# An order written by a planner: when scores, maxima and products with v take their turn on TensorE

## The chip, the cores and the metric

The kernel runs on one core of one Trainium2 chip. The metric is the device time of one execution in microseconds (us), as the median of several runs. The engines are named as in the profile: PE is TensorE (PEld its weight loads), DVE is VectorE, ACT is ScalarE, POOL is GpSimd, SP is SyncE, which here only issues DMAs.

## The reference

```python
xn = layernorm(x)                                  # x: (2, 2048, 256) float32
q = rope((xn @ wq).reshape(B, S, 16, 16))          # 16 heads of 16
k = rope((xn @ wk).reshape(B, S, 4, 16))           # 4 heads of keys and values
v = (xn @ wv).reshape(B, S, 4, 16)
k, v = repeat(k), repeat(v)                        # 4 query heads to each
scores = einsum('bshd,bthd->bhst', q, k) / 4, causal
out = einsum('bhst,bthd->bshd', softmax(scores), v) @ wo
y = real(ifft(fft(xn) @ (w_real + 1j * w_imag))) + bias
result = x + out + y
```

Everything is float32. The spectral term is a fixed 256 x 256 matrix, which the kernel builds once.

## The kernel before

The 4096 rows of x are cut into eight blocks of 512 rows (block n is batch n % 2, block row j = n // 2). A block has four *units* of four query heads each, 32 units in all. Unit u of block row j runs over 4 (j + 1) *steps*, one for every 128 keys; there are 320 steps. The work of a unit is of three kinds:

- *Maxima* (called "A" in the code, tiles `sm`). Before a softmax can be formed, the maximum of each row of scores is needed. PE multiplies queries by keys with the queries as weights (L155 for whole tiles, L627 and L631 with the causal mask), two heads to a tile of two PSUM banks, and DVE takes the maximum (`mx`, L636). There are two such tiles (`ps_s`, bufs=2). After a unit's last maximum, DVE splits the negated maxima into three bf16 parts (`parts`, L656), PE turns them (`spread`, "S", tile `ps_m`, L671), ACT copies them to `mt` (L677) and issues a DMA (L678) that puts them under the queries in `qst`, so that the next product subtracts the maximum by itself.
- *Scores* ("B", tiles `st`). PE multiplies again, with keys as weights (L155; L716 and L720 with the mask), one head at a time, four to a step, each into one PSUM bank. ACT takes the exponential into `es` in SBUF (L726). On the diagonal, POOL sets the masked part to zero (L729). There are three `st` banks (`ps_st`, bufs=3), and all smaller results that PE passes on (projections, turned tiles, outputs) go through the same three. `es` has 8 places, two to a step, so scores can be four steps ahead of the products.
- *Products with v* ("V", tile `av`, L757). For each step, four heads at once add to one PSUM bank (`ps_av`, bufs=1). `va` has a column of ones, so the sum of the exponentials comes along. After the last step of a unit ACT copies `av` to `avs` (`take`, L768), and only then can the next unit's first product begin. DMAs on the POOL queue then regroup the heads through DRAM (`put`, `gather`, `widen`), DVE inverts the sums and POOL scales.

Beside them stand the *pieces*: each block's load, row statistics, norm, turned rows (`ps_x`, L411), projections (`ps_q`, L155, evacuated by ACT at L427), rotation and split on POOL (L518 to L556), the DMAs that stack the parts into `qst` and `kst` (SP, L393), and each block's outputs (`po`, L155, added by DVE at L883). Each piece has a step from which it may be placed and a step by which it is due.

The order of all engines is written out at build time by a planner (`while True`, from L1070). It holds a clock for each engine (`clock`) and the time at which each value or free buffer is there (`there`), with costs for each operation: 0.22 us for a full score on PE and 0.49 on ACT, 0.87 for a product, 1.14 for a full maximum on DVE. At each turn it collects what could go next on PE, with the planned time at which it could begin (`at`). The choices that could begin within 0.05 us of PE's clock are in `soon`. A score needs a free `st` bank and, for the first of a pair, a free place in `es`. A maximum needs a free `sm` tile, and may be no more than six tiles (`WINDOW`) beyond those due at the next step. A piece that is due is "F", one that is not is "M". Then it picks:

```python
        act, dve = clock["act"] - pe, clock["dve"] - pe
        lag = now - v_next
        late = a_done < due[min(now, NS)]
        if not soon:
            pick = min(choices, key=lambda c: (c[0], "AFSBVM".index(c[1])))
        elif half and "A" in soon:
            pick = soon["A"]
        elif "S" in soon:
            pick = soon["S"]
        elif late and "A" in soon:
            pick = soon["A"]
        elif "F" in soon:
            pick = soon["F"]
```

`act` and `dve` are the work that ACT and DVE still have before them when PE comes to this turn; `lag` is how many steps the scores are ahead of the products. The branches that follow are those of the change, below. Each engine then runs its own list in the order in which it was written, and waits on semaphores for what it needs.

Of the kernel before, what the change touches and what calls it, by code (L numbers as in the profile page):

```python
# [23 lines left out]
def tile_attn_plus_spectral_ffn(  # L24
# [32 lines left out]
    B = x.shape[0]  # L57
# [42 lines left out]
    def take_slot(tag):  # L100
        used[tag] += 1
        return used[tag] - 1
# [5 lines left out]
    def ready(needs):  # L108

        if any(k not in there for k in needs):  # L110
            return None
        return max((there[k] for k in needs), default=0.0)
# [623 lines left out]
    def values_need(u, t):  # L736
        n, g = units[u]
        b, j = blocks[n]
        return [
            ("es", u, t, 0), ("es", u, t, 1), ("va", at_block[b, t // NI]), ("av", u - 1),  # L740
            *[("avs", u - 2)] * (t == (j + 1) * NI - 1),
        ]

    def values(u, t):
        n, g = units[u]
        b, j = blocks[n]
        nt = (j + 1) * NI
        if t == 0:
            av[u] = ps_av.tile([P, SB], F32, tag="av", name=f"av{u}")
            take_slot("av")  # L750
        lo = max(0, t - j * NI) * P
        use(
            "pe", (SB - lo) * 1.68e-3 + 0.01, values_need(u, t),
            [("es", es_slot[u, t, pr]) for pr in range(2)] + [("values", u)],
        )
        for h in range(NKV):
            nc.tensor.matmul(  # L757
                av[u][QD * h : QD * (h + 1), lo:],
                va[at_block[b, t // NI]][:, t % NI, h, :],
                es[u, t, h // 2][:, h % 2, lo:],  # L760
                start=(t == 0), stop=(t == nt - 1),
            )
# [3 lines left out]
    def take(u):  # L766
        avs[u] = work.tile([P, SB], F32, tag="avs", bufs=3, name=f"avs{u}")
        nc.scalar.copy(avs[u], av[u])  # L768
        take_slot("avs")
        use("act", 0.47, [("values", u), ("avs", u - 2)], [("av", u), ("avs", "in", u)])  # L770
# [125 lines left out]
    AHEAD = (3, 5, 5, 5)  # L896
    RATE = (1.4, 1.2, 1.12, 1.1)
    WINDOW = 6
    FULL = 0.7
    steps = [(u, t) for u, (n, g) in enumerate(units) for t in range((blocks[n][1] + 1) * NI)]  # L900
    first = {}
    for at, (u, t) in enumerate(steps):
# [41 lines left out]
    k = take_slot("st")  # L944
# [118 lines left out]
    def wants(needs, rings):  # L1063
        return [*needs, *(slot(*SECOND.get(tag, (tag, 0))) for tag in rings)]

    def start_of(eng, needs, rings=()):
        t = ready(wants(needs, rings))
        return None if t is None else max(t, clock[eng])

    while True:  # L1070
        now = b_next // NKV
        pe = clock["pe"]
        choices = []

        if now < NS:
            u, t = steps[now]
            h = b_next % NKV
            n, g = units[u]
            at = start_of(
                "pe", [("mt", n, g), ("kst", at_block[blocks[n][0], t // NI])],  # L1080
                ["st"] + ["es"] * (h % 2 == 0),
            )
            if at is not None:
                choices.append((at, "B", None))

        if v_next < NS and v_next < now:
            at = start_of("pe", values_need(*steps[v_next]))
            if at is not None:
                choices.append((at, "V", None))

        if a_done < len(a_list):
            at = pe if half else start_of("pe", a_list[a_done][2], ["s"])
            if at is not None and a_done < due[min(now + 1, NS)] + WINDOW:
                choices.append((at, "A", None))
        if spread_next < len(units) and ("np", *units[spread_next]) in there:
            at = start_of("pe", [("np", *units[spread_next])], ["st"])
            if at is not None:
                choices.append((at, "S", None))
        others = []
        for s in streams:  # L1100
            if s and (s[0][0] <= now or now >= NS):
                since, by, eng, needs, rings, what = s[0]
                at = start_of(eng, needs, rings)
                if at is None:
                    continue
                if eng == "pe":
                    choices.append((at, "F" if by <= now else "M", s))
                else:

                    if by <= now and ready(wants(needs, rings)) <= clock[eng] < pe + 1:  # L1110
                        at = min(at, pe)
                    others.append((at, s))
        limit = max(pe, min((c[0] for c in choices), default=1e9))
        if others and min(others, key=lambda c: c[0])[0] <= limit:
            soonest = min(others, key=lambda c: c[0])
            eng = soonest[1][0][2]
            s = min(
                (c for c in others if c[0] <= soonest[0] + 0.1 and c[1][0][2] == eng),
                key=lambda c: c[1][0][1],
            )[1]  # L1120
            s.pop(0)[-1]()
            continue
        if not choices:
            break
        soon = {}
        for c in choices:
            if c[0] <= pe + 0.05 and (c[1] not in soon or c[0] < soon[c[1]][0]):
                soon[c[1]] = c
# [10 lines that stand above are left out]
            pick = soon["A"]  # L1139
        elif "F" in soon:  # L1140
            pick = soon["F"]
        elif "B" in soon and act < FULL and (act <= dve or "A" not in soon):
            pick = soon["B"]
        elif "A" in soon and dve < FULL:
            pick = soon["A"]
        elif "V" in soon and lag > 1:
            pick = soon["V"]
        else:
            pick = next(soon[k] for k in "MVBA" if k in soon)
        kind = pick[1]  # L1150
        if kind == "B":
            scores(*steps[now], b_next % NKV)
            b_next += 1
            u, t = steps[now]
            if b_next % NKV == 0 and first[u + 1] == now + 1:
                n, g = units[u]
                there["qst", 2 + NG * n + g] = clock["pe"]
        elif kind == "V":
            values(*steps[v_next])
            v_next += 1  # L1160
            u = steps[v_next - 1][0]
            if first[u + 1] == v_next:
                take(u)
        elif kind == "A":
            one, two, needs, parts = a_list[a_done]
            (two if half else one)()
            if half:
                a_done += 1
                if parts:
                    parts()  # L1170
            half = not half
        elif kind == "S":
            made[spread_next][2]()
            spread_next += 1
        else:
            pick[2].pop(0)[-1]()
# [51 lines left out]
```

## Time and profile before

| | |
|---|---|
| median of 3 runs | 945.44 us (944.21 to 949.61) |
| profiled execution | 948.13 us, its span 946.4 us |
| granted PE clock | 0.996 |
| PE, DVE, ACT, POOL busy | 912.4, 751.8, 670.0, 370.8 us |
| scores on ACT (L726) | 1280 of 539 ns (mean of four widths) |
| maxima on DVE (L636) | 640 of 1058 ns (mean of four widths) |

The page of the profile gives busy time by engine, the busy share and the granted PE clock in 40 slices of the span, and the costliest groups of instructions. In a group's row, the first number after the bar is its busy time, the next the mean duration of one in ns, and after the second bar stands the time for which its engine was idle just before such instructions, with what ended most of that. [...]records of consecutive matmuls overlap, and four matmuls of 32 columns each run side by side.

### The profile page before, as it was taken

The numbers are of one execution on the slowest core, as the hardware profiler recorded it, in microseconds if no ns is written. First come the engines' busy times: TensorE is split into PE (matmuls) and PEld (weight loads), VectorE is DVE, ScalarE is ACT, GpSimd is POOL, SyncE is SP. The second block draws the span as 40 slices with busy tenths as digits, with TensorE's granted clock in tenths as the row PEclk, the third lists the DMA queues.
The fourth block names the chain that finished last, engine by engine and source line by source line (L and its number), as shares of the span: only waits on it lengthen the run. The fifth ranks groups of instructions, "written<-read, shape, count | busy, mean of one in ns | idle before, by whom it ended". The sixth has DMA issues, their size and how long they took to land.

```text
span 946.4 us, 39041 instructions
## 1 busy us (share of the span) xinstructions
PE 912.4 (96%) x17324; PEld 516.3 (55%) x17324; DVE 751.8 (79%) x1056; ACT 670.0 (71%) x1418; POOL 370.8 (39%) x556
## 2 busy tenths in 40 slices
PE   8998899999999999999999999999999999999996
PEld 5665665656565555655554555565456455555442
DVE  7777787789779995898897899879788887888511
ACT  3266555687667775888856777858688885888884
POOL 6397746825762324821337420302561031102201
PEclk9999999999999999999999999999999999999999
DMA  5436633350262011440012500010152001100000
GB/s 167 112 100 154 167 89 93 99 144 26 74 162 69 25 38 42 117 121 14 26 37 62 146 27 14 27 58 14 47 124 52 14 24 41 34 2 29 11 2 23
DMA packets 41993, 62.14 MB, mean 66 GB/s; under 512 B 8840, under 2 KB 32120, under 8 KB 41824
## 3 DMA queue, kind: packets, MB, share of 16 engines
q1 hardware_dynamic: 32400, 41.18, 16.4%
q0 software_dynamic: 8128, 17.69, 5.8%
q8 instruction: 135, 2.21, 1.0%
q10 hardware_dynamic: 1296, 0.79, 0.3%
q14 instruction: 34, 0.28, 0.1%
HBM read 32.75 MB, written 18.40 MB: 54 GB/s over the span
## 4 chain that ended last, share of the span: by engine, by line
PE 83%; ACT 6%; DVE 5%; issue 2%; POOL 2%; DMA 1%; ACTq 1%; POOLq 0%; DVEq 0%; SPq 0%
PE av L757 24%; PE st L155 21%; PE sm L155 16%; PE sm L631 6%; PE po L155 6%; ACT es L726 4%; PE ps_q L155 4%; DVE mx L636 3%; PE sm L627 2%; ACTq L678 1%; PE st L720 1%; ACT mt L677 1%; PE ps_x L411 1%; DMA run<-part 1%; PE st L716 1%
## 5 line engine op out<-in xcount | busy, mean ns | idle before, releaser
L726 ACT ACTIVATE es<-st 128x512 f32<-128x512 f32 (+3 forms) x1280 | 604.5, 539 | 194.5 <-PE st L155 154.3
L636 DVE TENSOR_REDUCE mx<-sm 128x2 f32<-128x1024 f32 (+3 forms) x640 | 652.6, 1058 | 107.6 <-PE sm L155 56.5
L155 PE MATMUL st<-qst,kst 115*32 115x512 bf16 (+3 forms) x4608 | 369.5, 353 | 11.1 <-ACT es L726 9.5
L757 PE MATMUL av<-es,va 128*32 128x512 f32 (+3 forms) x2560 | 302.1, 529 | 0.4
L155 PEld LDWEIGHTS <-kst 115*32 115x32 bf16 x4608 | 163.8, 95 | 152.4 <-issue 91.4
L155 PE MATMUL sm<-kst,qst 112*32 112x512 bf16 x3072 | 243.9, 380 | 1.4 <-DVE mx L636 0.8
L729 POOL TENSOR_SCALAR_AFFINE_SELECT es<-es 128x256 f32<-128x256 f32 x192 | 76.7, 406 | 312.1 <-ACT es L726 310.2
L155 PEld LDWEIGHTS <-qst 112*32 112x32 bf16 x3072 | 100.8, 96 | 83.4 <-issue 56.9
L631 PE MATMUL sm<-kst,qst 112*32 112x448 bf16 (+15 forms) x2048 | 123.6, 279 | 0.9 <-issue 0.5
L757 PEld LDWEIGHTS av<-es,va 128*32 128x32 f32 x2560 | 89.7, 110 | 35.5 <-ACT avs L768 2.6
L627 PE MATMUL sm<-mask,ident_h 128*32 128x96 bf16 (+3 forms) x2048 | 101.9, 201 | 4.8 <-DVE mx L636 3.2
L631 PEld LDWEIGHTS <-qst 112*32 112x32 bf16 x2048 | 68.4, 97 | 36.0 <-issue 22.6
L627 PEld LDWEIGHTS <-ident_h 128*32 128x32 bf16 x2048 | 67.4, 96 | 27.5 <-issue 22.0
L883 DVE TENSOR_TENSOR xr<-po,xr 128x256 f32<-128x256 f32 x36 | 15.2, 424 | 43.8 <-PE po L155 38.5
L155 PE MATMUL ps_q<-xnT,wp 128*32 128x512 f32 x384 | 44.7, 593 | 0.2 <-ACT xnT L414 0.2
L427 ACT COPY raw<-ps_q 128x512 f32<-128x512 f32 x24 | 14.1, 586 | 33.4 <-PE ps_q L155 29.3
L518 POOL TENSOR_TENSOR ra<-raw,cs 128x512 f32<-128x512 f32 (+1 forms) x21 | 27.4, 1304 | 23.2 <-ACT raw L427 22.0
L155 PE MATMUL po<-wo_sb,attT 128*32 128x256 f32 x512 | 35.5, 394 | 0.7 <-ACT attT L846 0.7
L720 PE MATMUL st<-qst,kst 115*32 115x512 bf16 (+14 forms) x512 | 35.2, 281 | 0.6 <-issue 0.6
L780 POOL DMA_DIRECT2D res<-avs x30 | 18.2, 607 | 44.2 <-ACT avs L768 44.2
L155 PE MATMUL po<-mff,xnT 128*32 128x256 f32 x512 | 33.9, 380 | 0.7 <-ACT es L726 0.6
L716 PE MATMUL st<-mask_t,ident_h 128*32 128x32 bf16 (+3 forms) x512 | 29.4, 203 | 3.5 <-ACT es L726 3.4
(106 smaller groups left out, 600.5 us busy)
## 6 DMA issues: line engine op xcount, KB each, us to landing
qst<-run SPq DMA_DIRECT2D x62, 128.0 KB
res<-avs POOLq DMA_DIRECT2D x30, 256.0 KB, 2.4
run<-part SPq DMA_DIRECT2D x31, 192.0 KB
qst<-run SPq DMA_DIRECT2D x31, 192.0 KB
xt<-in_L_attn_x_dram SPq DMA_DIRECT2D x8, 512.0 KB
xr<-in_L_attn_x_dram SPq DMA_DIRECT2D x16, 256.0 KB
out_dram<-xr SPq DMA_DIRECT2D x16, 256.0 KB
sw<-raw SPq DMA_DIRECT2D x60, 64.0 KB
```

Source lines behind the costliest of these rows:

```text
L155: nc.tensor.matmul(to[q : q + QD], lhsT[:, q : q + QD], rhs, start=start, stop=stop)
L518: e.tensor_tensor(ra[c][:r], raw[c][:r], cs[j][:r, 0, :], ALU.mult)
L627: nc.tensor.matmul(to[:, at:wd], ident_h[:, q : q + QD], mask[:, q:], start=True, stop=True, skip_group_check=True,)
L631: nc.tensor.matmul(to[:, : at + QD], rows[:, q : q + QD], keys[:, : at + QD], start=False, stop=True, skip_group_check=True,)
L636: nc.vector.tensor_reduce(t["mx"][:, i, 2 * pr : 2 * pr + 2, k], ps[0][:, :, :wd], AX.X, ALU.max)
L716: nc.tensor.matmul(to[:, lo : at + QD], ident_h[:, q : q + QD], mask_t[:, : q + QD], start=True, stop=True, skip_group_check=True,)
L720: nc.tensor.matmul(to[:, at:], keys[:, q : q + QD], rows[:, at:], start=False, stop=True, skip_group_check=True,)
L726: nc.scalar.activation(es[u, t, pr][:, e, lo:], ps[:, lo:], AF.Exp, scale=SCALE)
L729: nc.gpsimd.affine_select(out=es[u, t, pr][:, :, lo : lo + P], in_=es[u, t, pr][:, :, lo : lo + P], pattern=[[0, 2], [1, P]], compare_op=A ...
L757: nc.tensor.matmul(av[u][QD * h : QD * (h + 1), lo:], va[at_block[b, t // NI]][:, t % NI, h, :], es[u, t, h // 2][:, h % 2, lo:], start=(t ...
L780: nc.gpsimd.dma_start(out=res[n, c][f], in_=avs[u])
L883: nc.vector.tensor_tensor(xr[n, r][:, e, :], po, xr[n, r][:, e, :], ALU.add)
```

## The change

The bound FULL = 0.7 us on the work that ACT and DVE still have before them is taken out of the choice:

```diff
     WINDOW = 6
-    FULL = 0.7
...
         elif "F" in soon:
             pick = soon["F"]
-        elif "B" in soon and act < FULL and (act <= dve or "A" not in soon):
+        elif "B" in soon and (act <= dve or "A" not in soon):
             pick = soon["B"]
-        elif "A" in soon and dve < FULL:
+        elif "A" in soon:
             pick = soon["A"]
         elif "V" in soon and lag > 1:
             pick = soon["V"]
         else:
-            pick = next(soon[k] for k in "MVBA" if k in soon)
+            pick = soon["M"] if "M" in soon else soon["V"]
```

Before, a score was placed only while ACT had less than 0.7 us of planned work left, and a maximum only while DVE had less than that. With both above it, a product came next if the scores were more than one step ahead, else a piece not yet due, a product, and as the last resort a score or a maximum. Now a score or a maximum is placed whenever its buffers let it begin, and products and pieces not yet due come only when neither can. The set of instructions stays the same; their order changes on every engine. This is a stretch of PE's order in the middle of unit 27 before and after (s a score of one head, A a tile of maxima, V a product of one step, a point any other):

```
before  ssVAssAssAsVsAssVAssAssVAssAsVsAAssVsAsAssVsAsAssVsAsAssVsssAsAsV.ssAsAsAs
after   sAssVsAssAssVAssAssAVAssAssVAssAssVAssAssVAsssAsVAs.sVAssAsVsAssAssVsA
```

## The prediction, written before the result was known

> **What bounds the kernel now.** I read the page first: the busy shares, the clock row, and the costliest groups with their idle time.
>
> ```profile
> span 946.4 us, 39041 instructions
> ...
> PE 912.4 (96%) x17324; PEld 516.3 (55%) x17324; DVE 751.8 (79%) x1056; ACT 670.0 (71%) x1418; POOL 370.8 (39%) x556
> ...
> PEclk9999999999999999999999999999999999999999
> ...
> L726 ACT ACTIVATE es<-st 128x512 f32<-128x512 f32 (+3 forms) x1280 | 604.5, 539 | 194.5 <-PE st L155 154.3
> L636 DVE TENSOR_REDUCE mx<-sm 128x2 f32<-128x1024 f32 (+3 forms) x640 | 652.6, 1058 | 107.6 <-PE sm L155 56.5
> L155 PE MATMUL st<-qst,kst 115*32 115x512 bf16 (+3 forms) x4608 | 369.5, 353 | 11.1 <-ACT es L726 9.5
> L757 PE MATMUL av<-es,va 128*32 128x512 f32 (+3 forms) x2560 | 302.1, 529 | 0.4
> ```
>
> PE is the bound, at an almost full clock, and its idle time before scores and products is only some 11 us. But a matmul's record is longer than its turn, so a short wait hides inside "busy". The timeline near the end shows this (columns: start, duration, engine, line, operation, and the idle time before it with what ended it):
>
> ```profile
> 924.72 0.83 PE L155 MATMUL st<-qst,kst 115*32 115x512 bf16 x12
> 925.82 0.40 PE L155 MATMUL st<-qst,kst 115*32 115x512 bf16 x4 [0.26 <-ACT es L726]
> 926.03 1.04 PE L757 MATMUL av<-es,va 128*32 128x512 f32 x8
> 926.89 0.83 PE L155 MATMUL st<-qst,kst 115*32 115x512 bf16 x12
> 927.99 0.40 PE L155 MATMUL st<-qst,kst 115*32 115x512 bf16 x4 [0.26 <-ACT es L726]
> ```
>
> Four st matmuls (one score tile) take 0.21 us of PE (925.82 to 926.03), a product with v 0.86 (926.03 to 926.89). Three scores from 926.89 need 0.65, yet the fourth starts at 927.99, 1.10 after the first: 0.45 us lost, of which "idle" shows 0.26. The reason is the three st banks: the fourth score needs the first one's bank, that is 0.21 (its matmul), 0.235 until ACT starts, an exp record of 0.60, and 0.05 back to PE, 1.10 in all. Maxima are the same with two tiles:
>
> ```profile
> 700.34 0.62 PE L155 MATMUL sm<-kst,qst 112*32 112x512 bf16 x8
> 701.01 1.23 DVE L636 TENSOR_REDUCE mx<-sm 128x2 f32<-128x1024 f32 x1 [0.50 <-PE sm L155]
> ```
>
> PE spends 0.43 on a tile, DVE starts 0.24 after that and its record is 1.22; with 0.05 back, the second next tile can't start sooner than 1.51 us after the tile's end.
>
> So I summed PE's start-to-start times against the usual one for the same work (score 0.215, maxima tile 0.433, product 0.86). The work is 853 us, the lost time 89. 68 of it stands before scores and maxima: 19.0 before 155 us (scores 9.6, maxima 9.4), 38.4 from 155 to 886 (25.0 and 13.4), 10.2 after 886, where no maxima are left. Of the other 21, 3.8 follow the first idle matmuls, 5 are the closing chain, the rest lies around projections and outputs. The stages:
>
> ```profile
> 0.00:155.00 155.00, 141.66 (x3388) 90.94 (x3388) 121.38 (x250) 81.60 (x196) 100.08 (x142) 0.99 0.46 128
> 155.00:886.00 731.00, 721.91 (x13266) 403.13 (x13265) 622.13 (x786) 546.74 (x1135) 261.83 (x397) 1.00 0.20 57
> 886.00:947.00 61.00, 48.81 (x684) 22.26 (x676) 8.33 (x22) 41.64 (x89) 8.88 (x18) 0.96 0.03 10
> ```
>
> (Columns: PE, PEld, DVE, ACT, POOL busy, clock, DMA share, GB/s.) In no stage is another engine full; what PE loses, it loses to banks.
>
> **The change.** It adds and removes no instruction. It alters PE's order, and ACT's, DVE's, POOL's and SP's with it.
>
> 1. *The lead of the scores.* In the built order before, 189 of the 320 products stand with one step of scores ahead, 109 with two, 20 with three, 2 with four. After: 41, 89, 125, 65. With one step ahead a product is not ready when the banks fill, and PE takes a score or a maximum whose bank isn't free; with three there is always a product to put between.
>
> 2. *Bank waits.* In each order I counted the PE work (durations above) between the end of a tile and the tile that reuses its bank, and summed what lacks to 0.89 us (scores) or 1.51 (maxima; shorter tiles in proportion). Scores: early 4.6 to 2.4, middle 10.0 to 9.1, end 10.2 to 8.5. Maxima: 6.7 to 4.2, and 21.7 to 4.0. Together 53.2 to 28.2, so 25.0 less. For the order before the count stands beside 67.6 us in the trace (end 10.2 against 10.2), so it finds the right places. What it misses is a queue of several tiles. Looked for over up to 24 tiles back, the summed lack of maxima falls by 34% (119.5 to 78.4), of scores of the first three block rows by 3% (39.5 to 38.3). Lower bound of the gain: 34% of the 22.8 us that maxima lose in the trace is 7.8, 3% of the 34.6 of scores is 1.0, and 1.7 at the end: 10.5. Upper: 25.0. Middle: 17.7.
>
> 3. *The end.* After the last maximum PE has 40.4 us of work before and 43.4 after (25 products left, not 22), so that maximum comes 3 us earlier; the end gains only the 1.7 counted, as both orders still hold rows of four scores in sequence there.
>
> 4. *The copy of av (L768).* A unit's first product waits for it. It starts 0.76 us after the last product's matmuls (mean of 32), its record is 0.59, then 0.05: 1.4. PE work placed between the two products falls short of 1.34 by 3.3 us in sum before and 5.3 after: 2.1. With ACT fuller it could wait one exp (0.48) longer: short of 1.81 by 15.3, 12 us more. As a product lasts 1.8 exps and three banks hold at most three, I take 3 us.
>
> 5. *Pieces and queues.* Projections move by -3 to +6 us of PE work, outputs by -4 to +8, with their DMAs on SP, their POOL rotations and the stores; the final block's first products move back 7 us. Priced at nothing: between a block's last projection of a q half (c = 0) and its first maximum stand 43 to 47 us of PE work from block 3 on, 30 for block 2, against fourteen POOL steps (keys, then that half) of at most 1.3 us, 18, and two DMA hops of 2.8 and 2.5 in the chain of waits. Block 2 keeps 7 us of cover; if it went, PE would wait by what is short, once, as there are few other scores to place so early. The es ring gives no new wait on ACT: PE runs in order, the freeing product stands ahead of the score, and the exp comes 0.24 after that score.
>
> 6. *The clock.* The row: one window at half speed,
>
> ```profile
> 115.00:121.00 6.00, 5.39 (x128) 3.31 (x131) 3.05 (x3) 2.87 (x10) 3.46 (x7) 0.72 0.96 227
> ```
>
> which costs 1.7 us (6 x 0.28), and 1.00 through the middle with its 38 us of bank waits. The Trainium skill (TensorE: Matmul & The Clock Gate, "A second HAM failure mode: psum-queue depth-cycling") speaks against filling the banks: a PE that cycles through PSUM banks idles briefly and often, and its clock then swings between half and full. By that rule one half-speed window per unit would be 32 x 1.7 = 54 us; by the row it is 0. I take the row: waits this short didn't move the clock in 731 us.
>
> Sum: 17.7 - 3 = 14.7. The profiled execution takes 948.1 us (span 946.4), 2.7 above the median of the runs (945.4): from it 933.4, from the median 930.7, so 931 as the forecast.
>
> **The rivals.**
>
> *The waits come back (no change).* A removed bank wait gave ACT or DVE time to catch up; the next tile then waits. For it: over longer distances the scores' lack falls only 3%, and DVE works 85% of the middle stage. Against: the maxima's falls by a third. Gain 10.5 less all of item 4's 7 to 12: 943 to 945.
>
> *Copies behind the exps (slower).* Scores now fill all three banks before a product, so each copy of av stands behind one exp more, and the first product of the next unit holds up all PE work behind it: +12 us at 31 unit changes, while little of the bank gain arrives (3 us): 954. It decides where the copy starts over 1.2 us after the last product instead of 0.76. Against it: the product itself drains 1.8 exps.
>
> *The edit does little of what it says.* ACT's backlog seldom passed 0.7 in the planner, and the order would be nearly the same. The count of leads rules that out.
>
> **How the numbers follow.** Gain from bank waits 0.60, waits that come back 0.20, slower 0.20. Range 917 (all 25 counted, and some 3 of the waits around pieces) to 951 (half of the slower case). About 0.5% is what a measurement of this kernel can tell: faster means under 940.7, slower over 950.2. The gain case lies wholly below 940.7 but for its low end, which the lower end of the second case makes up for: 0.60, 0.20, 0.20. Its own range is 917 to 939.
>
> **What would show it.** Right: PE busy unchanged near 912 or lower in a span near 932; start-to-start loss before maxima in the middle under 8 us (13.4 before), the end stage still losing 8 to 10; copies of av under 1 us after the last product. Wrong: idle time "sm <- mx" or "st <- es" that grows; copies of av late; PEclk digits below 9 in the middle; idle time before maxima ended by a DMA, which would say that the pieces came late.

## The result and the profile after

The changed kernel takes 931.25 us (median of 4 runs, 929.02 to 932.66), beside 944.9 us of the kernel before (median of 4): a ratio of 0.984 (95% interval 0.981 to 0.988), so 1.6% faster. Run again later it came to 0.981 (0.979 to 0.983), 930.8 against 949.3. The profiled execution took 931.65 us with a span of 929.9. The page of the changed kernel, the lines that answer to those shown of before:

```profile
span 929.9 us, 39029 instructions
...
PE 906.8 (98%) x17324; PEld 500.6 (54%) x17324; DVE 748.5 (80%) x1056; ACT 657.1 (71%) x1418; POOL 370.1 (40%) x556
...
PEclk9999899999999999999999999999999999999999
...
L726 ACT ACTIVATE es<-st 128x512 f32<-128x512 f32 (+3 forms) x1280 | 592.3, 542 | 189.3 <-PE st L155 154.1
L636 DVE TENSOR_REDUCE mx<-sm 128x2 f32<-128x1024 f32 (+3 forms) x640 | 649.3, 1058 | 88.7 <-PE sm L631 45.9
L155 PE MATMUL st<-qst,kst 115*32 115x512 bf16 (+3 forms) x4608 | 353.2, 354 | 4.7 <-ACT es L726 3.5
L757 PE MATMUL av<-es,va 128*32 128x512 f32 (+3 forms) x2560 | 299.6, 530 | 0.9 <-POOL es L729 0.5
```

The counts of instructions of these five engines are the same, and so is the work; PE's share of the span rose from 96% to 98%. ACT and DVE are no busier in us. The stages, cut where the last maximum stands (columns: PE, PEld, DVE, ACT, POOL busy, clock, DMA share, GB/s):

```profile
0.00:155.00 155.00, 144.31 (x3396) 93.08 (x3400) 120.95 (x250) 81.81 (x197) 103.48 (x147) 0.98 0.48 132
155.00:869.00 714.00, 712.01 (x13232) 384.74 (x13228) 619.53 (x786) 532.35 (x1129) 257.70 (x392) 1.00 0.20 57
869.00:930.00 61.00, 50.51 (x708) 22.77 (x700) 7.99 (x21) 42.95 (x92) 8.92 (x18) 0.99 0.03 10
```

The middle stage shrank from 731 us to 714 and the end stage not at all: it has 3 us more of PE's work in it, as the prediction counted. The list of PE's waits of the middle stage shows which. Before (columns: what waited and for what, us in total, times, the longest):

```profile
PE st L155 <- ACT es L726: 4.8, 11, 0.6
PE sm L155 <- DVE mx L636: 0.8, 3, 0.3
PE sm L627 <- DVE mx L636: 0.7, 1, 0.7
PE ps_m L671 <- ACT es L726: 0.2, 1, 0.2
```

and after:

```profile
PE sm L627 <- DVE mx L636: 0.6, 1, 0.6
PE st L155 <- ACT es L726: 0.4, 2, 0.2
```

Only 6.5 us against 1.0, because this list sees idle time alone. By PE's start-to-start times, as in the prediction, the loss (us) is:

| lost before | scores, early | maxima, early | scores, middle | maxima, middle | scores, end | all else | sum |
|---|---|---|---|---|---|---|---|
| before | 9.6 | 9.4 | 25.0 | 13.4 | 10.2 | 21.1 | 88.7 |
| after | 11.1 | 5.7 | 21.9 | 6.9 | 8.8 | 18.5 | 72.9 |

The 15.8 us of difference are nearly the 16.5 us of the two spans. Maxima give 10.2 of it, scores 3.0, the rest 2.6.

These sums take every delay before a score or a maximum for a bank wait, and early in the run that isn't so. In the profiled execution of the changed kernel PE stands for 3.2 us in the middle of one masked score:

```profile
103.23 0.23 PE L716 MATMUL st<-mask_t,ident_h 128*32 128x32 bf16 x3
103.26 0.23 PE L720 MATMUL st<-qst,kst 115*32 115x128 bf16 x3
106.70 0.28 PE L716 MATMUL st<-mask_t,ident_h 128*32 128x128 bf16 x4 [3.20 <-issue]
```

Three of the score's four pairs of matmuls start at once, the fourth only at 106.70, although in the trace only the first matmul of a score has a wait of its own. The profile names no cause (the releaser "issue" means that PE waited for nothing that it shows), and the granted clock is 0.50 from 106 to 112 us. When the changed kernel was run again, its clock was 1.00 from 100 to 115 us, its longest stop of this kind was 1.1 us, and its scores lost some 3 us less early. So the rise of the early scores from 9.6 to 11.1 us doesn't come from banks.

The sum over scores hides two opposite movements. Once a unit, ACT copies `mt` and issues its DMA. This stretch of the kernel before (PE's rows, then ACT's) shows for unit 27's copy what that does:

```profile
723.54 0.27 PE L671 MATMUL ps_m<-ident_h,np 128*12 128x128 bf16 x2
723.65 0.54 PE L155 MATMUL st<-qst,kst 115*32 115x512 bf16 x5
723.88 0.75 PE L155 MATMUL sm<-kst,qst 112*32 112x512 bf16 x8
724.48 0.35 PE L155 MATMUL st<-qst,kst 115*32 115x384 bf16 x4
724.68 0.61 PE L155 MATMUL sm<-kst,qst 112*32 112x512 bf16 x8
725.91 0.35 PE L155 MATMUL st<-qst,kst 115*32 115x384 bf16 x4 [0.61 <-ACT es L726]
```

```profile
723.86 0.57 ACT L677 COPY mt<-ps_m 12x512 bf16<-12x512 bf16 x1 [0.24 <-PE ps_m L671]
724.46 0.76 ACTq L678 DMA_DIRECT2D qst<-mt  x1
725.26 1.36 ACT L726 ACTIVATE es<-st 128x512 f32<-128x512 f32 x3 [0.83 <-PE st L155]
```

From 723.86 to 725.26 ACT forms no exponential: 0.57 for the copy, then 0.76 for the DMA's issue, which the busy row doesn't count. PE has two maxima and two scores to place, then the third bank is missing, and no product is ready: the last maximum's matmuls take 0.43 of PE from 724.68, the next score starts at 725.91. The same copy in the changed kernel:

```profile
709.33 0.60 PE L155 MATMUL sm<-kst,qst 112*32 112x512 bf16 x5
709.68 0.68 PE L155 MATMUL st<-qst,kst 115*32 115x512 bf16 x8
710.11 1.11 PE L757 MATMUL av<-es,va 128*32 128x512 f32 x8
710.97 0.68 PE L155 MATMUL sm<-kst,qst 112*32 112x512 bf16 x8
```

```profile
709.53 0.57 ACT L677 COPY mt<-ps_m 12x512 bf16<-12x512 bf16 x1
710.14 0.75 ACTq L678 DMA_DIRECT2D qst<-mt  x1
710.94 2.08 ACT L726 ACTIVATE es<-st 128x512 f32<-128x512 f32 x4 [0.83 <-PE st L155]
```

ACT is away just as long, but a product (0.86 of PE, 710.11 to 710.97) stands in the gap, and PE doesn't stop. Over all such places after 155 us, 14 products start within 3 us of `ps_m` before, and 33 after. The scores in those 3 us lose 11.7 us before and 4.7 after. All other scores after 155 us lose a little more, 23.6 and 25.9.

### The profile page after: what moved, and what is told of

The parts are those of the page before. It is cut to its first block, busy times and chain, and to the rows that moved or that the text cites. A ratio compares the mean times of both kernels' runs of the same rounds, so it can differ in the third digit from the quotient of the medians.

```text
span 929.9 us, 39029 instructions
## 1 busy us (share of the span) xinstructions
PE 906.8 (98%) x17324; PEld 500.6 (54%) x17324; DVE 748.5 (80%) x1056; ACT 657.1 (71%) x1418; POOL 370.1 (40%) x556
## 3 DMA queue, kind: packets, MB, share of 16 engines
q1 hardware_dynamic: 32400, 41.18, 16.5%
## 4 chain that ended last, share of the span: by engine, by line
PE 88%; DVE 5%; ACT 3%; issue 1%; DMA 1%; POOL 1%; ACTq 0%; POOLq 0%; DVEq 0%
PE av L757 24%; PE st L155 23%; PE sm L155 17%; PE sm L631 7%; PE po L155 6%; PE ps_q L155 4%; ACT es L726 2%; DVE mx L636 2%; PE sm L627 2%; PE st L720 2%; PE ps_x L411 1%; PE st L716 1%; PE ps_m L671 0%; DMA xt<-in_L_attn_x_dram 0%; PE ps_sw L155 0%
## 5 line engine op out<-in xcount | busy, mean ns | idle before, releaser
L726 ACT ACTIVATE es<-st 128x512 f32<-128x512 f32 (+3 forms) x1280 | 592.3, 542 | 189.3 <-PE st L155 154.1
L636 DVE TENSOR_REDUCE mx<-sm 128x2 f32<-128x1024 f32 (+3 forms) x640 | 649.3, 1058 | 88.7 <-PE sm L631 45.9
L155 PE MATMUL st<-qst,kst 115*32 115x512 bf16 (+3 forms) x4608 | 353.2, 354 | 4.7 <-ACT es L726 3.5
L155 PE MATMUL sm<-kst,qst 112*32 112x512 bf16 x3072 | 239.0, 379 | 0.1
L155 PEld LDWEIGHTS <-qst 112*32 112x32 bf16 x3072 | 95.9, 96 | 93.1 <-issue 64.7
L631 PE MATMUL sm<-kst,qst 112*32 112x32 bf16 (+15 forms) x2048 | 122.6, 282 | 0.6 <-DMA qst<-part 0.6
L627 PE MATMUL sm<-mask,ident_h 128*32 128x64 bf16 (+3 forms) x2048 | 100.3, 201 | 1.1 <-DVE mx L636 0.9
L757 PEld LDWEIGHTS av<-es,va 128*32 128x32 f32 x2560 | 84.9, 110 | 28.2 <-issue 2.7
L631 PEld LDWEIGHTS <-qst 112*32 112x32 bf16 x2048 | 66.5, 97 | 34.0 <-issue 20.1
L627 PEld LDWEIGHTS <-ident_h 128*32 128x32 bf16 x2048 | 66.2, 96 | 32.9 <-issue 25.9
L720 PE MATMUL st<-qst,kst 115*32 115x480 bf16 (+15 forms) x512 | 37.2, 288 | 0.7 <-issue 0.7
L716 PE MATMUL st<-mask_t,ident_h 128*32 128x128 bf16 (+3 forms) x512 | 31.4, 205 | 4.4 <-issue 3.2
```

Of the source, the lines that this page charges most:

```text
L155: nc.tensor.matmul(to[q : q + QD], lhsT[:, q : q + QD], rhs, start=start, stop=stop)
L627: nc.tensor.matmul(to[:, at:wd], ident_h[:, q : q + QD], mask[:, q:], start=True, stop=True, skip_group_check=True,)
L631: nc.tensor.matmul(to[:, : at + QD], rows[:, q : q + QD], keys[:, : at + QD], start=False, stop=True, skip_group_check=True,)
L636: nc.vector.tensor_reduce(t["mx"][:, i, 2 * pr : 2 * pr + 2, k], ps[0][:, :, :wd], AX.X, ALU.max)
L716: nc.tensor.matmul(to[:, lo : at + QD], ident_h[:, q : q + QD], mask_t[:, : q + QD], start=True, stop=True, skip_group_check=True,)
L720: nc.tensor.matmul(to[:, at:], keys[:, q : q + QD], rows[:, at:], start=False, stop=True, skip_group_check=True,)
```

## The experiments

Three theories were set against each other. Theory 1: PE waits for banks of both kinds, less often when a ready product can be put between. Theory 2: a fuller ACT is what pays. Theory 3: it is the depth of the lead. The count in the expectations is that of the prediction, 53.2 us before and 28.2 after. Each ratio is to the kernel before on the same chip, which took 948 to 949 us there and not 945, so differences are compared and not the times expected.

**One bound at a time.** Only the scores':

```diff
-        elif "B" in soon and act < FULL and (act <= dve or "A" not in soon):
+        elif "B" in soon and (act <= dve or "A" not in soon):
```

> Only the bound on ACT's work is taken out (scores), that on DVE's work stays. Theory 1, bank waits as counted in the built order: the count of lacking time falls from 53.2 to 46.0 us only (maxima 28.4 to 21.9), and the full change paid 14 for 25 counted, so 4 us: 941. Theory 2, a fuller ACT (scores early) is what pays: nearly the whole gain, 932. Theory 3, the lead of the scores: 167 products with one step of lead or less become 141 against 41 after the full change, so little: 942.

940.1 us, ratio 0.991 (0.989 to 0.992): 8 us, twice the 4 of theory 1 and five short of the 13 of theory 2. What the count doesn't hold are the scores after an `mt` copy: there this order loses 6.8 us, 4.9 less than the order before. That is about the size of theory 1's miss; that it is the cause is read from the trace.

Only the maxima's:

```diff
-        elif "A" in soon and dve < FULL:
+        elif "A" in soon:
```

> Only the bound on DVE's work is taken out (maxima), that on ACT's work stays. Theory 1, bank waits: the count falls from 53.2 to 33.9, maxima from 28.4 to 12.5, so 11 us: 934. Theory 2, a fuller ACT pays: nothing of it is here, 945. Theory 3, the lead: 80 products with one step of lead (189 before, 41 after the full change), 4 with four: some three quarters of the gain, 935.

934.4 us, ratio 0.985 (0.983 to 0.986): 14 us, close to the whole effect. Theory 2 had said nothing, so a fuller ACT alone isn't what pays; theories 1 and 3 had said 11 and 10, and this run doesn't part them. Without the bound on DVE's work, maxima fill PE's time instead of products, the products fall back, and there is a ready one when it is needed: 80 products with a lead of one instead of 189. The two bounds don't add up: 8 and 14 alone, 14 to 18 together.

In these two runs the count has the wrong bank. With the scores' bound taken out, it put 6.5 of its 7.2 us at the maxima; by start-to-start times the loss before scores fell by about 9 us and that before maxima not at all. With the maxima's bound taken out, it put 15.9 of 19.3 us at the maxima; the loss before scores fell by about 12 us, that before maxima by about 6. So the count foretold that waits would go, but not at which kind of bank.

**The lead held at two.** The full change with one condition more:

```diff
-        elif "B" in soon and (act <= dve or "A" not in soon):
+        elif "B" in soon and lag < 2 and (act <= dve or "A" not in soon):
...
-            pick = soon["M"] if "M" in soon else soon["V"]
+            pick = next(soon[k] for k in "MVB" if k in soon)
```

> The full change, but a score is placed only while the scores are less than two steps ahead, so the lead is two at most nearly everywhere (106 products with one, 210 with two). Theory 1, bank waits: count 34.6 us, so 10 us: 935. Theory 2, a fuller ACT: the scores wait for products, most of the gain goes: 941. Theory 3, a deep lead of three to four steps is what pays: most of the gain goes, 942.

939.1 us, ratio 0.990 (0.988 to 0.992): 9 us, in six runs from 934.7 to 940.8. Theory 1's 10 is met, but the loss against the full change was also foreseen by theory 3 in kind, if larger. This run alone doesn't part them.

**A wider bound.**

```diff
-    FULL = 0.7
+    FULL = 1.1
```

> The bound stays on both, at 1.1 us instead of 0.7. Theory 1, bank waits: count 35.6 us, so 10 us: 935. Theory 2, a fuller ACT: half of the gain or more, 937. Theory 3, the lead: 64 products with one step, 50 with four: most of the gain, 934.

935.8 us, ratio 0.986 (0.984 to 0.987): 13 us. Most of the effect comes with 0.4 us more of planned backlog. Theory 1 had said 10, the others 8 and 11: it parts nothing.

**The change again, and with truer delays.** The second is the changed kernel with

```diff
-    LATE = {"pe": 0.2, "dve": 0.12, "act": 0.15, "pool": 0.12}
+    LATE = {"pe": 0.235, "dve": 0.14, "act": 0.17, "pool": 0.12}
```

> The changed kernel as it is, on the chip of the other three, so that they can be set beside it: 0.984 of the kernel before.

> The changed kernel with the planner's delays set to what the trace shows: PE to its reader 0.235 instead of 0.2, ACT back to PE 0.17 instead of 0.15, DVE back 0.14 instead of 0.12. Theory 1, bank waits: the count is 27.3 us against 28.2 (scores 20.0 to 18.1, maxima 8.2 to 9.2), so within 2 us of the changed kernel. Theory 3, the lead: 66 products with one step and 12 with four against 41 and 65, so 3 to 5 us slower than it.

930.8 us (0.981) and 930.9 us (0.981, 0.979 to 0.983): the same. In the second, 12 products have a lead of four instead of 65, and 179 of two instead of 89, and nothing is lost, where theory 3 had said 3 to 5 us. So it isn't depth as such. A lead of two seems enough if the product is placed where the bank would be missing; held at two by a rule that looks at no bank, it gave 9 of 14 to 18 us. That the placing makes this difference was not tested by itself.

**Making the readers faster.** Here orders and PE's work are kept, and part of DVE's and ACT's work is left out. The maxima:

```diff
-                        t["mx"][:, i, 2 * pr : 2 * pr + 2, k], ps[0][:, :, :wd], AX.X, ALU.max
+                        t["mx"][:, i, 2 * pr : 2 * pr + 2, k], ps[0][:, :, : wd // 2], AX.X, ALU.max
```

The exponentials (the product's `rhs` then reads the written half twice, and POOL masks only what is written):

```diff
-        nc.scalar.activation(es[u, t, pr][:, e, lo:], ps[:, lo:], AF.Exp, scale=SCALE)
+        hw = lo + (SB - lo) // 2
+        nc.scalar.activation(es[u, t, pr][:, e, lo:hw], ps[:, lo:hw], AF.Exp, scale=SCALE)
```

> The kernel before, in its own order, with each of the 640 maxima taken over the first half of its columns only, so that a full one lasts some 0.68 us instead of 1.22 and the tiles come free half a microsecond sooner. PE's work and its order stay. Theory 1, bank waits: the 22.8 us that stand before maxima go, and some of them turn up before the next score: 15 to 20 us faster, 929 to 934 of 948. Rival, PE's waits come from the order of pieces or the end: under 5 us faster.

> The changed kernel, in its own order, with the same halved maxima. Theory 1, bank waits: 12.6 us stand before maxima in the trace of the changed order, so 8 to 12 us faster than it, 921 to 925 on this chip, and the distance between the two orders falls from 15 us to 5 to 8, since what sets them apart is mostly the wait for DVE. Rival, the gain lies in pieces or the end: the distance stays at 14 to 15.

> The kernel before, in its own order, with each exponential formed over the first half of its columns only (a full one lasts some 0.39 us instead of 0.60), and the products reading that half twice, so that PE's work and order stay. Theory 1, bank waits of both kinds: 44.8 us stand before scores; most go, a quarter turns up before maxima, as the halved maxima sent theirs to the scores: 20 to 25 us faster, 924 to 929 of 949. Rival, ACT's time doesn't matter since PE is the bound: under 5 us faster.

> The changed kernel, in its own order, with the same halved exponentials. Theory 1: 41.8 us stand before its scores, so 15 to 22 us faster than the changed kernel, 909 to 916. If it is the score waits in which the two orders differ once DVE is out of the way, the distance of 18 us between the orders shrinks to 10 to 14. Rival, the distance lies outside the banks: it stays.

> The kernel before, in its own order, with maxima and exponentials both halved. Theory 1: waits can no longer move from one kind of bank to the other; what stays is PE's work of 853 us, the start, the closing chain and the waits around pieces, some 40: 900, that is 49 us faster. Rival: the halves add up to no more than each alone, under 30 us.

> The changed kernel, in its own order, with both halved. Theory 1: both orders come to the same time, 897 to 902, since they have the same work and no banks to wait for: distance under 5 us. Rival, the order of pieces or the end carries the gain: the distance stays at 14 to 18 us.

| | order before: us, ratio | changed order: us, ratio | distance |
|---|---|---|---|
| as they are | 949.3, 1 | 930.8, 0.981 | 1.9% |
| maxima halved | 941.2, 0.992 | 927.6, 0.978 | 1.4% |
| exponentials halved | 932.1, 0.983 | 917.0, 0.967 | 1.6% |
| both halved | 914.2, 0.964 | 903.6, 0.953 | 1.1% |

The intervals of the ratios are 0.0015 to 0.0025 to either side. The last two rows come from another chip than the first two; the kernel before took 948.3 us there. The costliest groups show that the edit did its part: a full maximum took 691 ns instead of 1218, a full exponential 383 instead of 603.

```profile
L636 DVE TENSOR_REDUCE mx<-sm 128x2 f32<-128x512 f32 x448 | 305.9, 691 | 261.3 <-PE sm L155 201.5 <-PE sm L631 45.7 <-PE st L155 12.2
L727 ACT ACTIVATE es<-st 128x256 f32<-128x256 f32 x896 | 306.8, 383 | 275.3 <-PE st L155 260.7 <-PE st L720 4.6 <-POOL es L730 2.1
```

(The first row is of halved maxima, the second of halved exponentials, both in the order before.)

Halved maxima gave 8 us where 15 to 20 were expected: by start-to-start times the loss before maxima fell from 22.8 to 6.4, but that before scores rose from 44.8 to 54.3. More than half of what was taken away came back at the other kind of bank. With halved exponentials the loss before scores fell to 22.5 and that before maxima rose to 31.0. That gave 16 us where 20 to 25 were expected. Both together gave 34 us by the ratio, the sum of the two alone is 24. In the changed order the halved maxima gave 3 us of 8 to 12 expected and the halved exponentials 14 (by the ratios) of 15 to 22, and the distance between the orders stayed near 14 and 15 us, more than expected in both. So the two kinds of wait stand in for each other, as theory 1 says, only more strongly than expected. It also explains why the maxima's 10.2 us of the main result can't be put down to DVE alone: the product placed between spares both.

The last expectation, that both orders would meet within 5 us, failed: 10.6 us stayed, between the 5 of theory 1 and the 14 to 18 of its rival. PE's waits, with both halved, by the list (order before, then the changed order):

```profile
PE st L155 <- ACT es L727: 5.5, 13, 0.9
PE st L716 <- ACT es L727: 1.5, 4, 0.6
```

```profile
PE st L155 <- ACT es L727: 1.3, 5, 0.4
```

The loss before maxima is now 4.8 and 4.1, that before scores 28.5 and 19.9; of these, scores within 3 us of an `mt` copy lose 9.9 and 2.3. Scores and maxima together differ by 9.3 us, and the two profiled spans by 9.4 (911.4 and 902.0), so pieces carry none of what stayed. Some 7.6 us of it stand behind the one stay of ACT that was not halved. That this stay is their cause is read from the traces; a run that takes it off ACT was not made.

No version tried is faster than the changed kernel with the work complete.

## Why the prediction was right

- *The bound.* Right. PE was and is the bound. Its loss in the middle sat in short bank waits that the idle column hides. Early, "it loses to banks" says too much: there the order before also has the 1.7 us of half-speed clock of step 6 and 2.3 us of stops before scores and maxima with the releaser "issue".
- *Bank waits (step 2), lower bound 10.5, upper 25.0, middle 17.7.* The loss before scores and maxima fell by 13.2 us. The middle was 4.5 too high, of which the stop in the middle of a score may account for some 3. By stage: early 2.2 against 4.7 counted, middle 9.6 against 18.6, end 1.4 against 1.7.
- *Maxima and scores within that.* The lower bound took 34% of the maxima's 22.8 us; their loss fell by 10.2, or 45%. For scores it took 1.0 outside the end, and 1.6 came; but as the sum of 7.0 less after an `mt` copy, 1.5 more early (the stop) and the rest more in the other scores of the middle. So this agreement is luck. The count knew tiles and banks, and not that ACT leaves for 1.4 us once a unit: this is the term that it left out.
- *The end (step 3).* Right: the last maximum came 17.3 us earlier where the span shrank by 16.5, so what follows it grew by 0.8, where step 3 makes it 1.3 (3 more of work, 1.7 less of waits). The loss of the end fell from 10.2 to 8.8, and there are still four scores in sequence there. The changed kernel's end has the same 0.26 us of idle before every fourth score:

```profile
894.87 0.83 PE L155 MATMUL st<-qst,kst 115*32 115x512 bf16 x12
895.97 0.40 PE L155 MATMUL st<-qst,kst 115*32 115x512 bf16 x4 [0.26 <-ACT es L726]
896.18 1.05 PE L757 MATMUL av<-es,va 128*32 128x512 f32 x8
```

- *The copy of av (step 4), 3 us of loss.* Mis-sized: it cost nothing. The copy starts 0.79 us after a unit's last product instead of 0.76, and what products wait fell from 3.6 to 3.0 us. So two errors, 4.5 too much of gain and 3 too much of loss, largely cancelled, and 2.6 us of gain came that were priced at nothing. The forecast of 931 came closer than its terms, and that part is luck.
- *Pieces (step 5) and the clock (step 6).* Priced at nothing: the loss before all else but scores and maxima fell by 2.6. The clock stood at 1.00 in the middle stage with 28.8 us of bank waits, as it had with 38.4. The rule that the prediction cites, that PE's clock swings when it cycles through PSUM banks, did not decide here. Early in the run the mean clock is 0.77 from 100 to 115 us (the digit 8), twice what the one half-speed window took before; that is 1.7 us more at most, as PE stood still in part of it, and the repeat had none.
- *The rivals.* "The waits come back" was right as a mechanism: the halved maxima show it. It took half of the count, not all. Its 943 to 945 us don't follow from its terms, though: item 4 has 3 or 12 us and no 7, and a gain of 10.5 less 7 to 12 would be 942 to 947. "Copies behind the exps" is refuted by the 0.79 us.

## What to carry to other kernels

Where an engine runs its list in order and is the bound, as PE here, a placing rule is worth something if it has work ready to run when a buffer is not yet free: let the work that needs no fresh bank fall two or three steps behind, and spend it where the wait would be. Look for such waits in start-to-start times and not in idle time, since overlapping records (0.38 us for a matmul of 512 columns, at 0.215 from score to score) hide those under 0.17 us and the first part of longer ones. A start-to-start sum in turn holds whatever delays PE, banks or not: look at the largest pieces one by one. Before pricing one wait, ask what would be late next: here half of what one reader stopped costing was paid at the other.

## What the runs showed of the hardware

- In the kernel before, a stop of ACT that no busy row holds: the `mt` copy and the issue of its DMA from ACT's queue keep ACT from its next exponential for 1.40 us (723.86 to 725.26), of which the copy is 0.57.
- From the end of a tile's turn on PE to the reader's start 0.235 us, and 0.05 from the end of the reader's record to PE's next matmul in that bank; with a 0.60 us exponential this makes 0.89 us. With three banks PE loses what its own work between the two uses of a bank falls short of that: 0.45 us for four scores in sequence at the end.
- Halved in columns, an exponential takes 383 ns instead of 603 and a maximum 691 instead of 1218: by a straight line through the two, an estimate, some 160 ns of each don't depend on the columns.
